# Cross-attention block on one core: all eight W1 blocks by seven products, W2's products summed in shared PSUM banks, joint norm statistics

## The chip, the cores and the metric

The kernel runs on one core of one Trainium2 chip. The metric is device time in microseconds (us) of one execution; the number to predict is the median over several runs. The kernel before has a median of 1502.2 us over three runs (1501.49 to 1502.87).

## The reference: what is computed

`x` and `ctx` hold 128 batches of 128 tokens with 256 features, all float32. There are 16 heads of 16 features, and the feed-forward width is 1024. For each batch:

```python
q = split(x @ Wq + bq);  k = split(ctx @ Wk + bk);  v = split(ctx @ Wv + bv)     # 16 heads
scores = q @ k.T / 4;    scores[j >= i] = -1e30;    attn = softmax(scores)
attn[:, :, 0, :] = 0                                 # row 0 sees nothing
x1  = layer_norm(x + (attn @ v) @ Wo + bo) * g1 + be1
out = layer_norm(x1 + relu(x1 @ W1 + b1) @ W2 + b2) * g2 + be2
```

## The kernel before

Work goes by **pairs** of batches: 64 pairs `p`, 256 tokens each. A pair's way takes six software-pipelined stages, and `step(p)` runs, for `p` = 7 to 63, one stage each of several pairs. On the PE (TensorE) one step does in this order: `weigh(p-2)` (probabilities times values, PSUM tile `pc`), `scores_both(p)` (`pss`), `queries(p+1)` (`pq`), `attention_out(p-2)` (`po`), the keys of `p+1` (`pk`), `values(p)` (`pv`), then `second_by_seven(p-4)` (W2) and `hidden_by_seven(p-3)` (W1). The prologue (`third` to `sixth`) fills the pipeline. Step 63 is the `last` one; its W1 is plain (`hidden`), and behind it `behind(62)`, `behind(63)` and the closing lines run the pairs that are left.

**What sets the order.** The program is put out under a manual schedule: each engine runs its instructions in the order in which the code issues them, and waits by semaphores where a tile is not ready. So where a call stands in `step` decides where its instructions stand in every engine's queue. VectorE is DVE, ScalarE ACT, GpSimd POOL; SP and sometimes ACT issue DMAs.

**Seven products.** A 2x2 block product needs eight block matmuls done plainly. `second_by_seven` (L809) and `hidden_by_seven` (L898) use a Strassen-like scheme: seven products of sums of blocks, with a chain of additions behind. For W2 the sums of the hidden activations are `hS` (`combine_hidden`, POOL, L795 to L798), the sums of weights are `wt`. The seven products go to two PSUM banks, `py` (bank 6, four of them) and `pz` (bank 7, three), each product with four matmuls of 128 columns and with `empty` NOPs between them. When all are done, `sum_of_seven` (DVE, L838 and L846) adds them in five instructions to the residual `x1b` and gives `t2`. For W1, `combine_normed` makes the sums `xS` of the normed tokens (POOL, L866 to L869) and `w1t` holds the weights' sums. The 1024 columns of W1 are eight blocks of 128, four pairs of blocks; `NI = 3` of the pairs go by seven products (21 matmuls of 128 columns, each product in a bank of its own), and blocks 6 and 7 go plainly (L939, four matmuls of 256 columns). The results are added on DVE (`u2`, `u3`, `add2`, `add3`, `add5`: L910 to L924), and ACT applies bias and ReLU block by block. In the profile every float32 matmul shows as two PE instructions, so a product of W2 is a row of `x8`, one of W1 a row of `x6`.

**Round about.** `sums(p, hi, part)` is a reciprocal on DVE (L433) and a normalising multiply on POOL (L434); `turn` transposes the probabilities on DVE (L447), and `bring` moves them by DMA. `turn_x1` transposes the normed tokens (L674) and issues `x1t` and `x1T`, two DMA trips in a row; `combine_normed` waits for `x1T`. Layer-norm statistics are taken for pair `p-2` (first norm) and `p-5` (second norm) apart: each `stats` (L536, L537) on DVE, then `deviation` (L543, L544) and `shift` (L588) on POOL. `residual1` (POOL, L577 and L580) makes `x1b`; `finish` (L608 and L609) closes the second norm.

Of the kernel before, what the change touches and what calls it, by code (L numbers as in the profile page):

```python
# [8 lines left out]
F32 = mybir.dt.float32  # L9
# [4 lines left out]
P = 128  # L14
# [5 lines left out]
def tile_cross_attention_block(  # L20
# [99 lines left out]
    def row(v, name):  # L120
        t = const.tile([P, v.shape[1]], F32, tag=name, name=name)
        nc.sync.dma_start(t, v.to_broadcast([P, v.shape[1]]))
        return t

    load_tokens(0, slice(0, 2))
# [9 lines left out]
    power = const.tile([P, 2, 1], F32, tag="power", name="power")  # L135
# [4 lines left out]
    table = const.tile([P, 2, 1], F32, tag="table", name="table")  # L140
# [11 lines left out]
    be1_r = row(ln1_b, "be1_r")  # L152
    b2_r = row(b2, "b2_r")
# [132 lines left out]
    def copy_keys(p):  # L286
        st = states[p]
        pk = st.pop("pk")
        for m in range(KC):
# [131 lines left out]
    def sums(p, hi, part):  # L421
# [11 lines left out]
        nc.vector.reciprocal(rs, su)  # L433
# [5 lines left out]


# [98 lines left out]
    def deviation(p, i):  # L539
# [4 lines left out]
        nc.gpsimd.tensor_tensor(sd, ve, power, ALU.pow)  # L544
# [28 lines left out]
    def residual1(p, engine=nc.gpsimd):  # L573

        st = states[p]
        x1b = st["x1b"] = ffn.tile([P, 2, D], F32, tag="x1b", name=f"x1b_{p}", bufs=3)
# [46 lines left out]
    b1s = const.tile([P, DFF // NS], F32, tag="b1s", name="b1s")  # L623
# [47 lines left out]
    def turn_x1(p, queue=nc.sync):  # L671
        st = states[p]
        tb = ffn.tile([P, NS, 4 * 32], F32, tag="tbx", name=f"tbx_{p}")
# [63 lines left out]
    def second_sum(p):  # L737
        st = states[p]
        t2 = st["t2"] = ffn.tile([P, 2, D], F32, tag="t2", name=f"t2_{p}", bufs=3)
        nc.vector.tensor_tensor(  # L740
            t2, st.pop("py").rearrange("p (s d) -> p s d", s=2), st.pop("x1b"), ALU.add
        )
# [36 lines left out]
    wt = const.tile([P, 4, FC // 2, P], F32, tag="wt", name="wt")  # L779

    def combine_w2():

        w = w2.rearrange("p (k e) (h d) -> p e h k d", e=2, h=2)
# [16 lines left out]
    def second_by_seven(p):  # L800

        st = states[p]
        hT, hs = st["hT"], st["hS"]
        py = st["py"] = at_bank(6, f"py_{p}")
        pz = st["pz"] = at_bank(7, f"pz_{p}")

        def product(out, left, right, after):
            for k in range(FC // 2):
                nc.tensor.matmul(  # L809
                    out, left(k), right(k), start=(k == 0), stop=(k == FC // 2 - 1)  # L810
                )
                empty(after // (FC // 2) + (after % (FC // 2) > k))

# [6 lines left out]
        product(py[:, :P], raw(0, 0), weights(0, 0), 5)  # L820
        product(pz[:, :P], raw(1, 0), weights(1, 0), 5)
        product(pz[:, 2 * P : 3 * P], raw(1, 1), lambda k: wt[:, 3, k], 5)
# [531 lines left out]
    def step(p):  # L1354
# [55 lines left out]
        if not last:  # L1410
            turn(p, 1, 1)
# [128 lines left out]
```

## Time and profile before

| | before |
|---|---|
| median of three runs | 1502.2 us |
| span of the profiled execution | 1500.2 us |
| mean granted TensorE clock | 0.999 |
| PE busy | 1487.9 us, 99% of the span |
| POOL, DVE, ACT busy | 1357.8, 1334.8, 1290.5 us |

The three runs' times are device times; the profiled execution is shown by its span, from the first to the last instruction, and has no other time of its own on record. The median lies 2.0 us above the span. A step of the steady part lasts 22.80 us, and 56 whole steps (`p` = 7 to 62) lie between 143.54 and 1420.82 us. In the page's rows `xN` counts instructions, the first number behind the bar is busy time, the second the mean duration in ns, and what follows the second bar is idle time before them and its releaser.

### The profile page before, as it was taken

The page shows a single profiled execution, that of the slowest core. Times are in us where ns is not written, and L with a number is a line of the kernel's source. Part 1 is how long each engine was busy: PE and PEld are TensorE (multiplying, and loading weights), DVE is VectorE, ACT ScalarE, POOL GpSimd, SP SyncE. Part 2 cuts the span into 40 slices and gives each one's busy share as a digit, 9 for nine tenths or more (in the row PEclk, how much of TensorE's full clock was granted, in tenths as well). Part 3 has the DMA queues.
Part 4 walks back from the last instruction along what each step waited for, and adds up shares of the span by engine and source line. Part 5 has one row for each costly group of instructions (what it writes and reads, how often), then busy time and mean ns, then how long its engine had stood idle before and what let it go on. Part 6 is the DMA issues. An engine that isn't in the chain of part 4 may idle for free.

```text
span 1500.2 us, 53576 instructions
## 1 busy us (share of the span) xinstructions
PE 1487.9 (99%) x18934; PEld 1366.7 (91%) x18934; DVE 1334.8 (89%) x2663; ACT 1290.5 (86%) x5271; POOL 1357.8 (91%) x1510
## 2 busy tenths in 40 slices
PE   8999999999999999999999999999999999999998
PEld 7788999999999999999999999999999999999997
DVE  6989998998999999999999989989999999899875
ACT  5658988989989989989989899899899899898862
POOL 6878899999999999999999999999999999999983
PEclk9999999999999999999999999999999999999999
DMA  8356656556666566556556565666665565564451
GB/s 200 84 113 143 149 140 137 139 141 140 149 138 142 135 139 145 143 128 146 142 130 156 137 139 136 139 141 147 140 137 139 131 157 142 128 143 128 107 136 49
DMA packets 415317, 204.61 MB, mean 136 GB/s; under 512 B 282449, under 2 KB 383057, under 8 KB 415057
## 3 DMA queue, kind: packets, MB, share of 16 engines
q1 hardware_dynamic: 412768, 199.34, 56.9%
q8 instruction: 158, 2.59, 0.8%
q10 hardware_dynamic: 2288, 1.85, 0.5%
q14 instruction: 103, 0.84, 0.2%
HBM read 70.26 MB, written 33.29 MB: 69 GB/s over the span
## 4 chain that ended last, share of the span: by engine, by line
PE 93%; DVE 3%; POOL 2%; DMA 1%; issue 1%; ACT 1%; SPq 0%; ACTq 0%; POOLq 0%; DVEq 0%
PE phs L898 18%; PE py L809 14%; PE pz L809 10%; PE pq L261 8%; PE pv L301 7%; PE po L523 7%; PE pk L261 7%; PE ph L939 6%; PE pss L384 6%; PE pc L504 4%; PE pc L494 2%; PE ph L710 2%; POOL sm L434 1%; PE py L730 0%; DVE sm L398 0%
## 5 line engine op out<-in xcount | busy, mean ns | idle before, releaser
L775 ACT ACTIVATE sm<-pss,nmx 128x128 f32<-128x128 f32 x944 | 327.8, 402 | 82.5 <-DVE nmx L758 75.5
L434 POOL TENSOR_TENSOR sm<-sm,rs 128x1024 f32<-128x1024 f32 x192 | 361.8, 1899 | 36.4 <-DVE rs L433 33.4
L775 ACT ACTIVATE sm<-sm,nmx 128x64 f32<-128x64 f32 x944 | 313.4, 401 | 0.0
L447 DVE STREAM_TRANSPOSE tb<-sm 128x1024 f32<-128x1024 f32 x186 | 228.1, 1229 | 22.4 <-POOL sm L434 12.0
L775 ACT ACTIVATION_READ_ACCUMULATOR sm<-sm,nmx 128x1 f32 x912 | 231.8, 254 | 0.0
L775 ACT ACTIVATION_READ_ACCUMULATOR sm<-pss,nmx 128x1 f32 x912 | 221.6, 243 | 0.0
L929 ACT ACTIVATE hT<-hT,b1e_c 128x256 f32<-128x256 f32 x336 | 152.1, 501 | 37.0 <-DVE hT L917 37.0
L809 PE MATMUL py<-wt,hS 128*128 128x128 f32 x1440 | 170.7, 275 | 0.0
L809 PEld LDWEIGHTS py<-wt,hS 128*128 128x128 f32 x1440 | 165.6, 192 | 0.0
L758 DVE TENSOR_REDUCE nmx<-pss 128x4 f32<-128x512 f32 x236 | 150.5, 678 | 0.0
L398 DVE TENSOR_TENSOR sm<-pss,neg 128x256 f32<-128x256 f32 (+1 forms) x276 | 107.9, 433 | 40.5 <-PE pss L384 38.9
L898 PE MATMUL phs<-xS,w1t 128*128 128x128 f32 x1008 | 130.9, 275 | 0.0
L291 ACT ACTIVATE kT<-pk,bkh,half 128x256 f32<-128x256 f32 x252 | 123.4, 605 | 4.0 <-PE pk L261 4.0
L261 PE MATMUL pq<-xT,wq 128*128 128x256 f32 x504 | 125.4, 392 | 0.0
L523 PE MATMUL po<-wo,cxT 128*128 128x256 f32 x512 | 121.3, 380 | 0.7 <-ACT cxT L516 0.7
L898 PEld LDWEIGHTS phs<-xS,w1t 128*128 128x128 f32 x1008 | 121.6, 192 | 0.0
L301 PE MATMUL pv<-wv,cT 128*128 128x256 f32 x512 | 121.0, 379 | 0.0
L261 PE MATMUL pk<-cT,wk 128*128 128x256 f32 x504 | 119.2, 379 | 0.0
L523 PEld LDWEIGHTS po<-wo,cxT 128*128 128x128 f32 x512 | 96.9, 190 | 14.5 <-ACT cxT L516 1.3
L301 PEld LDWEIGHTS pv<-wv,cT 128*128 128x128 f32 x512 | 97.2, 190 | 13.2
L261 PEld LDWEIGHTS pq<-xT,wq 128*128 128x128 f32 x504 | 90.7, 189 | 20.2 <-issue 9.8
L261 PEld LDWEIGHTS pk<-cT,wk 128*128 128x128 f32 x504 | 95.7, 190 | 13.1 <-issue 0.2
(165 smaller groups left out, 4085.0 us busy)
## 6 DMA issues: line engine op xcount, KB each, us to landing
pT<-tb SPq DMA_DIRECT2D x976, 96.0 KB, 2.2
x1t<-tbx SPq DMA_DIRECT2D x252, 64.0 KB, 2.9
x1T<-x1t SPq DMA_DIRECT2D x63, 256.0 KB, 3.0
out_dram<-t SPq DMA_DIRECT2D x63, 256.0 KB, 3.2
xb<-in_x_dram SPq DMA_DIRECT2D x124, 128.0 KB, 4.3
cb<-in_ctx_dram SPq DMA_DIRECT2D x124, 128.0 KB, 3.8
x<-in_x_dram SPq DMA_DIRECT2D x31, 512.0 KB, 4.7
w<-in_L_xattn_W_dram SPq DMA_DIRECT2D x2, 1024.0 KB, 8.2
```

The costliest lines, as they stand in the source:

```text
L261: nc.tensor.matmul(ps[:, m * TP : (m + 1) * TP], w[:, k, m * P : (m + 1) * P], src[:, k, :], start=(k == 0), stop=(k == KC - 1),)
L291: nc.scalar.activation(st["kT"][:, m, e, :], pk[:, m * TP : (m + 1) * TP], AF.Identity, bias=bkh[:, m, e : e + 1], scale=half[:, e : e + 1],)
L301: nc.tensor.matmul(pv[:, s * D : (s + 1) * D], st["cT"][:, k, s * P : (s + 1) * P], wv[:, k, :], start=(k == 0), stop=(k == KC - 1),)
L398: nc.vector.tensor_tensor(st["sm", hi][:, 4 * r : 4 * r + 4, :], st["sps", hi][r][:, : 4 * n].rearrange("p (n j) -> p n j", j=n), no[:, No ...
L434: nc.gpsimd.tensor_tensor(sm[:, part, :], sm[:, part, :], rs[:, :, None].to_broadcast([P, part.stop - part.start, n]), ALU.mult,)
L447: nc.vector.transpose(st["tb"][:, :, at : at + 256].rearrange("p j (n a) -> p n j a", a=32), st["sm", hi].rearrange("p h j -> p (h j)")[:, ...
L523: nc.tensor.matmul(po[:, s * D : (s + 1) * D], cxT[:, k, s, :], wo[:, k, :], start=(k == 0), stop=(k == KC - 1),)
L758: nc.vector.tensor_reduce(st["nmx", 1][:, 4 * r : 4 * r + 4], st["sps", 1][r].rearrange("p (n j) -> p n j", j=P), AX.X, ALU.max, negate=True,)
L775: nc.scalar.activation(sm[:, h, :], src, AF.Exp, bias=nmx[:, h : h + 1], scale=1.0, **({"accum_out": st["su", hi][:, h : h + 1]} if summed ...
L809: nc.tensor.matmul(out, left(k), right(k), start=(k == 0), stop=(k == FC // 2 - 1))
L898: nc.tensor.matmul(ps[:, i * P : (i + 1) * P].rearrange("p (n a) -> p n a", a=32), left(i), right, start=True, stop=True,)
L929: nc.scalar.activation(self.hT[:, f], self.plains.get(f, self.hT[:, f]), AF.Relu, bias=b1e_c[:, f : f + 1], scale=1.0,)
```

## The change

- `NI` is 4: all eight W1 blocks go by seven products, 28 matmuls of 128 columns; the plain part is gone. The order of the products is 1, 6, 7, 5, 2, 4, 3. Products 5 and 3 share PSUM bank 2: DVE reads it after 5 (`add5`) and once more after 3 was accumulated onto it (`add3`). Product 4 is in bank 7.
- W2's seven products share three banks: `px` (bank 6) takes three, `py` (bank 7) two, `pz` (bank 3) two side by side. DVE reads a bank midway, before the next product is accumulated onto it, and adds each part at once to the residual tile `t2`, which takes the place of `x1b`: six instructions instead of five.
- The statistics of both norms are one block, `both_stats`: four `bn_stats`, four `bn_aggr`, one `tensor_scalar` and one `scalar_tensor_tensor` on DVE, one power on POOL.
- The order changes: the transposes of the tokens and probabilities stand between the partial sums, `combine_normed` stands ahead of `sums` on POOL, two of the ReLUs go to the start of the next step, and 21 NOPs a step stand where there were 34.
- Some constants share the space of `wt`; `tbx` has one buffer, `t2` four.

```diff
-        def product(out, left, right, after):
+        def product(out, left, right, after, sums, first=False):
             for k in range(FC // 2):
                 nc.tensor.matmul(
-                    out, left(k), right(k), start=(k == 0), stop=(k == FC // 2 - 1)
+                    out, left(k), right(k), start=(first and k == 0), stop=(k == FC // 2 - 1),
+                    skip_group_check=True,
                 )
                 empty(after // (FC // 2) + (after % (FC // 2) > k))
+            for part in sums:
+                others.get(part, lambda: None)()
+                sum_of_seven(p, part)
...
-        product(py[:, :P], raw(0, 0), weights(0, 0), 5)
-        product(pz[:, :P], raw(1, 0), weights(1, 0), 5)
-        product(pz[:, 2 * P : 3 * P], raw(1, 1), lambda k: wt[:, 3, k], 5)
-        product(py[:, 3 * P :], lambda k: hs[:, 0, k], lambda k: wt[:, 0, k], 5)
-        product(py[:, 2 * P : 3 * P], lambda k: hs[:, 2, k], lambda k: wt[:, 2, k], 5)
-        product(py[:, P : 2 * P], lambda k: hs[:, 1, k], lambda k: wt[:, 1, k], 5)
-        product(pz[:, P : 2 * P], lambda k: hs[:, 3, k], weights(1, 1), 4)
+        product(px, raw(0, 0), weights(0, 0), 3, (), True)
+        product(py, lambda k: hs[:, 0, k], lambda k: wt[:, 0, k], 3, (), True)
+        product(pz[:, :P], raw(1, 0), weights(1, 0), 3, (0,), True)
+        product(px, lambda k: hs[:, 1, k], lambda k: wt[:, 1, k], 3, (1,))
+        product(pz[:, P : 2 * P], raw(1, 1), lambda k: wt[:, 3, k], 3, (2,))
+        product(py, lambda k: hs[:, 3, k], weights(1, 1), 3, (3, 4))
+        product(px, lambda k: hs[:, 2, k], lambda k: wt[:, 2, k], 3, (5,))
+    def sum_of_seven(p, part):
+        t = st["t2"].rearrange("p s (h d) -> p (s h) d", h=2)
+        to, of = {
+            0: (t[:, 0], "px"), 1: (t[:, 3], "py"), 2: (t[:, 1], "px"), 3: (t[:, 0:3:2], "pz"),
+            4: (t[:, 1], "py"), 5: (t[:, 2:], "px"),
+        }[part]
...
+        nc.vector.tensor_tensor(to, to, of, ALU.add)
-    NI = 3
+    NI = 4
-        WHERE = {1: 2, 6: 3, 7: 4, 4: 5, 2: 6, 3: 0, 5: 1}
+        WHERE = {1: 2, 6: 5, 2: 6, 7: 3, 4: 7}
+        ONTO = {3: 5}
+        AGAIN = {5: 2}
@@ hidden_by_seven
         h.run(1)
         h.run(6)
         h.keep()
+        copy_keys(p + 1, (1,))
+        h.again()
+        h.u2()
+        spread_values(p)
         stack_values(p)
-        h.u2()
         h.run(7)
-        h.run(4)
+        h.run(5)
         h.u3()
         norm1(p - 2)
+        h.add5()
         h.run(2)
         h.add2()
+        h.run(4)
         h.run(3)
-        h.run(5)
+        norm2(p - 5)
+        h.add4()
         h.relu(0)
         h.relu(2)
         h.relu(4)
-        h.add3()
-        h.add5()
-        h.plain([6], 2)
         h.relu(6)
         turn_x1(p - 2)
-        h.plain([7], 3)
-        norm2(p - 5)
-        h.relu(1)
-        h.relu(7)
+        h.add3()
+        turn(p, 0, 0)
@@ step, the last one (p = 63)
+            sums(p, 1, ONE)
+            sums(p, 1, TWO)
+            shift(p - 5, 2)
+            turn_x1(p - 2)
+            turn(p, 1, 0)
+            second_by_seven(p - 4)
+            residual1(p - 3)
+            sums(p, 0, ALL)
+            turn(p, 1, 1)
+            hidden(p - 3, range(FC))
@@ step, all others
+        joint = both_stats(p)
         sums(p, 1, ONE)
         sums(p, 1, TWO)
+        nc.gpsimd.tensor_tensor(joint[1], joint[1], power, ALU.pow)
+        second_by_seven(p - 4, {
+            1: lambda: (tokens(p + 2, "x") if ahead else None, turn(p, 1, 0)),
+            2: lambda: tokens(p + 2, "c") if ahead else None,
+            3: lambda: (reciprocal(p, 0, ALL), turn(p, 1, 1)),
+            5: lambda: both_shifts(*joint),
+        })
```

Three places show what this does to the engines' queues. The first is the PE at the end of W1 in a steady step, up to the first matmul of the next step's `weigh` (`pc`); `phs_N` is product N of W1 (product 3 runs in the tile of 5), `ph` the plain part, and the brackets name the semaphores waited for. Before:

```order
L898 MATMUL phs_3_12176<-xS_12034,w_127 128x128 [waits Activation_49,Pool_49]
L898 MATMUL phs_3_12176<-xS_12034,w_127 128x128 x2
L898 MATMUL phs_5_12180<-xS_12034,w1t 128x128 [waits Activation_49]
L898 MATMUL phs_5_12180<-xS_12034,w1t 128x128 x2
L939 MATMUL ph_6_12189<-x1T_11802,w_127 128x256 [waits PE_49]
L939 MATMUL ph_6_12189<-x1T_11802,w_127 128x256
L939 MATMUL ph_7_12202<-x1T_11802,w_127 128x256 [waits DVE_49]
L939 MATMUL ph_7_12202<-x1T_11802,w_127 128x256
L494 MATMUL pc_12230<-pT_11820,vd_178 32x64 [waits DMAHW4_49,DMAHW5_49,DMAHW3_49,DMAHW6_49,DMAHW2_49,DMAHW7_49,DMAHW1_49,DMAHW0_49]
```

And in the changed kernel:

```order
L934 MATMUL phs_5_11580<-xS_11381,w1t 128x128 [waits Activation_49]
L934 MATMUL phs_5_11580<-xS_11381,w1t 128x128 x3
L934 MATMUL phs_2_11566<-x1T_11250,w_128 128x128 [waits DVE_49]
L934 MATMUL phs_2_11566<-x1T_11250,w_128 128x128 x3
L934 MATMUL phs_4_11568<-x1T_11250,w1t 128x128 x4
L934 MATMUL phs_5_11580<-xS_11381,w_128 128x128 [waits DVE_49,Pool_49]
L934 MATMUL phs_5_11580<-xS_11381,w_128 128x128 x3
L506 MATMUL pc_11650<-pT_11262,vd_177 32x64 [waits DMAHW4_49,DMAHW3_49,DMAHW5_49,DMAHW2_49,DMAHW6_49,DMAHW1_49,DMAHW7_49,DMAHW0_49,DVE_49]
```

The plain matmuls are gone, each product has a fourth matmul, and `pc` also waits for DVE: its bank 7 holds product 4 until `add4` has read it.

The second place is the PE within W2 of the same step, from the third to the fourth product. Before, the fourth product stands at the place of the first that uses `hS`:

```order
L809 MATMUL py_12067<-wt,hS_11932 128x128 [waits Pool_49]
L215 NO_OP x2
L809 MATMUL py_12067<-wt,hS_11932 128x128
L215 NO_OP
L809 MATMUL py_12067<-wt,hS_11932 128x128
```

In the changed kernel, where `pX` is the tile that three products share:

```order
L842 MATMUL pz_11490<-w_134,hT_11192 128x128
L842 MATMUL pX_11488<-wt,hS_11376 128x128 [waits DVE_49,Pool_49]
L218 NO_OP
L842 MATMUL pX_11488<-wt,hS_11376 128x128
L218 NO_OP
```

The fourth product, D in what follows (A to G in the order of the new code), now waits for DVE too: the first partial sum must have read `pX` before it.

The third place is DVE in the last step, `p` = 63. Before:

```order
L433 RECIPROCAL rs_63_0_24224<-sa_63_24141 128x8
L433 RECIPROCAL rs_63_8_24227<-sa_63_24141 128x8
L674 STREAM_TRANSPOSE tbx_24233<-x_61_24204 128x4x4x32
L447 STREAM_TRANSPOSE tb_24242<-sm_24087 128x8x4x32
L838 TENSOR_TENSOR t_59_24311<-x1b_23935,py_24244 128x512
L838 TENSOR_TENSOR t_59_24311<-t_59_24311,py_24244 128x384
L838 TENSOR_TENSOR t_59_24311<-t_59_24311,py_24244 128x256
L838 TENSOR_TENSOR t_59_24311<-t_59_24311,py_24244 128x2x128
L846 TENSOR_TENSOR t_59_24311<-t_59_24311,pz_24245 128x384
```

And in the changed kernel:

```order
L439 RECIPROCAL rs_63_0_22986<-sa_63_22903 128x8
L439 RECIPROCAL rs_63_8_22989<-sa_63_22903 128x8
L706 STREAM_TRANSPOSE tbx_22995<-x_61_22966 128x4x4x32
L459 STREAM_TRANSPOSE tb_23004<-sm_22849 128x8x4x32
L878 TENSOR_TENSOR t_59_22701<-t_59_22701,pX_23006 128x128
L878 TENSOR_TENSOR t_59_22701<-t_59_22701,py_23007 128x128
L878 TENSOR_TENSOR t_59_22701<-t_59_22701,pX_23006 128x128
L878 TENSOR_TENSOR t_59_22701<-t_59_22701,pz_23008 128x2x128
L878 TENSOR_TENSOR t_59_22701<-t_59_22701,py_23007 128x128
L878 TENSOR_TENSOR t_59_22701<-t_59_22701,pX_23006 128x256
```

The sums stand behind the same two transposes as before; what is new is that the first three of them have to come before products D, F and G.

219 lines of the change are left out of this document (104 added, 115 removed).

## The prediction

> **What bounds the kernel now.** I read the page first, then the table of windows over the steady part, then PE's timeline of one step, then the chain of waits at the end.
>
> ```profile
> span 1500.2 us, 53576 instructions
> PE 1487.9 (99%) x18934; PEld 1366.7 (91%) x18934; DVE 1334.8 (89%) x2663; ACT 1290.5 (86%) x5271; POOL 1357.8 (91%) x1510
> PE 93%; DVE 3%; POOL 2%; DMA 1%; issue 1%; ACT 1%; SPq 0%; ACTq 0%; POOLq 0%; DVEq 0%
> ```
>
> PE is busy 99% of the span and makes up 93% of the chain that ended last. The next rows are windows: the 56 steady steps, then one step cut at the start of its W1.
>
> ```profile
> 143.54:1420.82 1277.28, 1277.27 (x16688) 1187.24 (x16688) 1161.99 (x2351) 1162.43 (x4928) 1195.80 (x1343) 1.00 0.60 139
> 736.80:753.08 16.28, 16.28 (x249) 15.16 (x249) 15.09 (x32) 14.94 (x75) 15.39 (x15) 1.00 0.52 131
> 753.08:759.60 6.52, 6.52 (x53) 6.03 (x51) 5.68 (x12) 5.82 (x16) 5.99 (x11) 1.00 0.82 147
> ```
>
> The columns are length, then busy PE, PEld, DVE, ACT, POOL, the granted clock, DMA. PE is busy 1277.27 of 1277.28 us, so a steady step (1277.28 / 56 = 22.81, 22.80 in this one) is as long as PE's own work; DVE, ACT and POOL each leave 1.4 to 2.1 us of it. So only work taken from PE, or a wait put into PE, moves the time. I write times in a step as an offset from `pc`'s start (here 736.80).
>
> **W1.** PE's timeline of the step:
>
> ```profile
> 729.39 1.06 PE L809 MATMUL pz<-w,hS 128*128 128x128 f32 x8
> 730.28 0.83 PE L898 MATMUL phs<-x1T,w 128*128 128x128 f32 x6
> 734.97 1.89 PE L939 MATMUL ph<-x1T,w 128*128 128x256 f32 x8
> 736.80 0.43 PE L494 MATMUL pc<-pT,vd 128*32 128x64 f32 x16
> 743.38 1.89 PE L261 MATMUL pk<-cT,wk 128*128 128x256 f32 x8
> 745.11 1.89 PE L301 MATMUL pv<-wv,cT 128*128 128x256 f32 x8
> 746.83 1.05 PE L809 MATMUL py<-w,hT 128*128 128x128 f32 x8
> ```
>
> Seven products are 42 PE instructions and take 734.97 - 730.28 = 4.69, or 0.1117 each. The plain part is 8 instructions at (745.11 - 743.38) / 8 = 0.216, or 1.73. Together 6.42; the window is 6.52, so 0.10 is lost at the passage to `pc`. In the change W1 is 56 instructions, 56 x 0.1117 = 6.255; with the same 0.10 it is 6.355. PE saves 0.165 a step and the step falls to 22.64, unless a wait comes in; 56 x 0.165 = **9.2 us**. The NOPs taken out are worth nothing: a W2 product with five of them takes (730.28 - 729.39) / 8 = 0.111 per instruction, what a W1 product takes without any.
>
> **The other engines.** Groups by line and form:
>
> ```profile
> L846 DVE TENSOR_TENSOR t<-t,pz 128x384 f32<-128x384 f32 x60 | 33.2, 554 | 6.8 <-DVE t L838 0.9
> L838 DVE TENSOR_TENSOR t<-t,py 128x256 f32<-128x256 f32 x120 | 50.5, 421 | 4.1
> L536 DVE BATCH_NORM_STATS2 bs<-t 128x6 f32<-128x256 f32 x254 | 101.9, 401 | 2.3
> L537 DVE BATCH_NORM_AGGREGATE mv<-bs 128x2 f32<-128x6 f32 x254 | 46.2, 182 | 8.7
> ```
>
> and one row of DVE's timeline, an addition of 512 columns out of PSUM:
>
> ```profile
> 745.38 0.68 DVE L549 TENSOR_TENSOR t<-po,xb 128x512 f32<-128x512 f32 x1
> ```
>
> The joint statistics take a power, two additions and four products, all a few columns wide, from POOL and give DVE two such instructions. POOL leaves 1.4 us of a step, and PE never stands still in it, so this is worth nothing by itself; what it can do is bring POOL's later work forward. From 384 to 256 columns a sum falls by 0.133, so I put a 128-column part at 0.29: the six parts are 4 x 0.29 + 2 x 0.42 = 2.0 where the five sums were some 2.6. W1's additions grow from 0.55 to 0.68 (384 to 512 columns). DVE stays near 21 of 22.64, ACT is the same but for 0.1. No engine but PE becomes the bound by its work.
>
> **The new waits of a steady step.** Four places on PE now wait for DVE. A starts at offset 10.03 and a product is 0.89, so D is due at 12.7, F at 14.5, G at 15.4. These rows time the inputs:
>
> ```profile
> 740.58 1.27 POOL L795 TENSOR_TENSOR hS<-hT 128x512 f32<-128x512 f32 x1
> 745.61 1.26 POOL L254 TENSOR_TENSOR xb<-x,bov_r 128x512 f32<-128x512 f32 x1
> 747.43 3.75 POOL L434 TENSOR_TENSOR sm<-sm,rs 128x1024 f32<-128x1024 f32 x2 [0.56 <-DVE rs L433]
> 751.14 0.45 POOL L866 TENSOR_TENSOR xS<-x1T 128x128 f32<-128x128 f32 x1
> 741.64 0.38 SPq L242 DMA_DIRECT2D x1T<-x1t  x1
> x1T<-x1t SPq DMA_DIRECT2D x1, 256.0 KB, 3.0
> 749.87 2.59 DVE L447 STREAM_TRANSPOSE tb<-sm 128x1024 f32<-128x1024 f32 x2 [0.22 <-DMA pT<-tb]
> ```
>
> - D waits for part 0. DVE has `t1` by 9.3, the joint statistics take 4 x (0.40 + 0.18) = 2.3, part 0 ends at 11.9: slack 0.8.
> - F waits for part 1, behind the probabilities' transpose, which waits for POOL. POOL starts `hS` at 3.8 to 3.9 and is through its four at 8.9 (745.61 - 740.58 = 5.03). `combine_normed` now stands there and needs `x1T`: issued at 4.84, landing 3.0 later at 7.9, so no wait; it is done at 10.7, the first multiply at 12.6, the transpose (2.59 / 2) at 13.9, part 1 at 14.3. Slack 0.2.
> - G waits for part 2, one token transpose (512 columns, some 0.6 by the 2.59 for 2048) and 0.29 later than part 1, at 15.2: slack 0.2.
> - `pc` waits for `add4`. Product 4 is the sixth of seven: its last instruction starts at 16.28 + 47 x 0.1117 = 21.53 and lasts 0.28 (row below), `add4` takes 0.68: 22.5, against 22.64. Slack 0.1.
>
> ```profile
> L898 PE MATMUL phs<-xS,w1t 128*128 128x128 f32 x1008 | 130.9, 275 | 0.0
> ```
>
> No row has these waits, so I bound them: no stall at all, or, if each hand-over takes 0.1 more than I allow, up to 0.13 at `pc`, 7.3 us in all. A stall at F, G or `pc` holds back all that PE does next, in the order `pc`, `pss`, `pq`, so it comes back every step. I take no stall, as all four slacks are positive; the gain lies between 1.9 and 9.2.
>
> **The last step.** Here the new waits are not short. Rows of PE, DVE and POOL around it:
>
> ```profile
> 1430.15 2.84 PE L809 MATMUL py<-wt,hS 128*128 128x128 f32 x24
> 1433.72 7.07 PE L710 MATMUL ph<-x1T,w 128*128 128x256 f32 x32
> 1434.24 3.75 POOL L434 TENSOR_TENSOR sm<-sm,rs 128x1024 f32<-128x1024 f32 x2
> 1434.16 0.71 DVE L674 STREAM_TRANSPOSE tbx<-x 128x512 f32<-128x512 f32 x1 [1.47 <-ACT x L565]
> 1436.17 1.25 DVE L447 STREAM_TRANSPOSE tb<-sm 128x1024 f32<-128x1024 f32 x1 [1.30 <-POOL sm L434]
> ```
>
> D is due at 1430.15. But on DVE the parts stand behind two transposes, of which one waits for ACT until 1434.16 and one for POOL until 1436.17; it ends at 1437.42. Part 0 ends at 1437.71, and D starts at 1437.75: PE stands still for **7.6 us**. Before, the same order cost nothing, since PE waited for no sum and went on with L710. Everything behind it on PE (three products, W1 of pair 60, the epilogue) moves by that, and it isn't given back: PE's rows from there to its last matmul follow each other nearly without a gap.
>
> Behind it the same waits cost less. Rows of the end:
>
> ```profile
> 1439.69 2.62 ACT L718 ACTIVATE hT<-ph,b1e_c 128x256 f32<-128x256 f32 x7
> 1474.16 1.22 PE L809 MATMUL py<-w,hT 128*128 128x128 f32 x8
> 1475.23 0.70 DVE L795 TENSOR_TENSOR hS<-hT 128x512 f32<-128x512 f32 x1 [1.20 <-ACT hT L718]
> 1477.17 0.69 DVE L798 TENSOR_TENSOR hS<-hT,hS 128x512 f32<-128x512 f32 x1
> 1480.71 1.53 PE L710 MATMUL ph<-x1T,w 128*128 128x256 f32 x6
> ```
>
> In `behind(62)`, part 0 stands behind four `hS` and the statistics of pair 59: the ReLUs, now right behind PE, end 1.1 after W1; the four `hS` take some 2.6 (1475.23 to 1477.86 in a later row), the statistics 2 x (0.40 + 0.18) = 1.2, part 0 0.3: 5.1, where D is due 4.2 after W1: **+0.9**. In `behind(63)` ACT's eight DMA issues hold the time and I put the change at **-0.2**. In the closing W2, B needs the first `hS`, done at 1475.93, 0.9 behind its due time of 1475.05; and part 0 comes behind the last `hS` (1477.86). That is D at 1478.2 where it would be 1476.84, less the 0.3 that this W2 already loses (1480.71 - 1474.16 = 6.55 against 6.25): **+1.0**.
>
> **The clock behind a long pause.** The last matmul starts from `py_last` (first row); the windows are of the tail; the last row is from the start:
>
> ```profile
> 1487.69 7.07 PE L1491 MATMUL py_last<-w,hT 128*128 128x256 f32 x32
> 1497.00:1498.50 1.50, 0.00 (x0) 0.00 (x0) 0.41 (x1) 0.00 (x0) 0.00 (x0) 1.00 0.13 46
> 1498.50:1500.20 1.70, 0.00 (x0) 0.00 (x0) 0.00 (x0) 0.00 (x0) 0.00 (x0) 0.53 0.12 42
> 6.59 3.78 PE L984 MATMUL pk<-cT,wk 128*128 128x256 f32 x8
> ```
>
> PE ends at 1494.76; the granted clock is 1.00 until 1498.50, 3.7 us on, and 0.53 after. At the start, behind idle time, 8 instructions take 3.78 where they take 1.89 later: half pace for about 3.6 us (6.59 to 10.17). A pause of 7.6 us is past that 3.7, so I add half of 3.6, **+1.8**; between 0 (no loss on return) and 5 (half of the program's first 10.2 us, if half pace held all that time).
>
> The Trainium skill's page "TensorE: Matmul & The Clock Gate", Part 1, states the same gate: after an idle window of about 3.4 us the clock passes every second pulse, until the PE was busy for such a window again. By its figure the pause would cost an estimated 1.7 us, and its table of rules speaks against any pause over some 3 us between bursts, as this change makes one. The trace agrees as to the fall (3.7 us); no row of it shows a return in the midst of a program, and the clock column reads 1.00 at the start, where the matmuls take twice as long.
>
> **The sum.** 1500.2 - 9.2 + 7.6 + 0.9 - 0.2 + 1.0 + 1.8 = 1502.1. The prologue (four sums of W1's weights a third wider, on POOL) I put at nothing, as POOL runs ahead there. The median of runs lies 2.0 above the profiled span, so **1504.1 us**. What this kernel's measurement can tell from no change is 0.2%, 3.0 us: 1499.2 to 1505.2.
>
> **Rivals.**
> 1. *The midway chain is late in each steady step.* F has 0.2 of slack behind five links (`hS`, `x1T`, `combine_normed`, multiply, transpose), `pc` 0.1 behind `add4`. It decides from the point where the links together take 0.25 more than summed. At 0.4 more, 0.2 x 56 = 11.2 are lost: 1515. For it: POOL now has `combine_normed` and two multiplies in a row ahead of the transpose, and the `x1T` landing varies with the DMA load. Against it: POOL's 5.99 of 6.52 in W1 came from work that is now elsewhere or gone. Chance 0.15; with half of it, 1510.
> 2. *The stall at 63 is smaller or made up for.* If ACT's and POOL's rows came 5 us earlier, or the epilogue absorbed it, 1504.1 - 7.6 - 1.8 = 1494.7. Against it: the two releasers do not depend on W2. Chance 0.07.
> 3. *The 0.10 at the passage to `pc` goes away too*, as the matmuls ahead of it are narrow now: 56 x 0.10 = 5.6 more, 1498.5. For it: this is the only gap in the step. Against it: the same passage stays (a narrow 32-row `pc` behind full tiles), with one wait more. Chance 0.13.
> 4. *The clock does not fall*: 1502.3. Chance 0.15.
>
> My forecast has 0.50: gain and loss nearly cancel. Within it, the small stalls at `pc` (0 to 7.3) and the upper bound of the clock reach up to 1511, so a good third of it lies above 1505.2. Alone it would be 1502 to 1509. Range: from 1496 (most of rival 3 and part of 2) to 1512 (half of rival 1). Faster: rivals 2 and 3 and a little, 0.22. Slower: rival 1 (0.15) and 0.2 of the forecast's, 0.35. Same: 0.43.
>
> **What would show it.** Right: 56 steps of 22.64 with PE busy throughout, W1 at 6.36, and one pause of 7.6 on PE in the last step, released by DVE's first partial sum, with a lower granted clock behind it. Wrong: PE waits for DVE at F or `pc` in each step (rival 1); no pause, or a short one, near 1430 (rival 2); W1 at 6.26 (rival 3); full pace right behind the pause (rival 4).

## The result, and the profile after

The changed kernel takes 1528.43 us in the median of four runs (1526.44 to 1529.95); the kernel before 1501.85, also in four. The ratio is 1.0178, 95% interval 1.0164 to 1.0193: **1.8% slower**, where I had forecast no change (1504.1). The profiled span is 1526.8 us, 26.6 above that of before.

The page of the changed kernel, its head and its chain:

```profile
span 1526.8 us, 53815 instructions
PE 1500.5 (98%) x19270; PEld 1387.0 (91%) x19270; DVE 1368.1 (90%) x2835; ACT 1313.8 (86%) x5271; POOL 1258.1 (82%) x1118
PE 92%; DVE 3%; ACT 1%; issue 1%; POOL 1%; DMA 1%; SPq 0%; POOLq 0%; DVEq 0%; ACTq 0%
```

This looks like before, and it misleads: PE seems as busy as it was, though it has less to do. Cutting the program at the starts of `pc` (from the trace's records) shows where the time went:

| us | before | after | difference |
|---|---|---|---|
| up to the start of step 7 | 143.54 | 144.10 | +0.6 |
| 56 steps (7 to 62) | 1277.3 | 1292.8 | +15.5 |
| the last step (63) | 19.90 | 29.06 | +9.2 |
| pair 62's stage behind it | 16.63 | 17.32 | +0.7 |
| the rest | 42.86 | 43.52 | +0.7 |

The end, from the last step on, is 10.5 us longer; the forecast's terms for it make 11.1. The start says little: over the kernels of this study it varies from 141.25 to 144.69. The steady part is not as forecast: I had it 9.2 us faster, and it is 15.5 slower. One steady step in windows (length, busy PE, PEld, DVE, ACT, POOL, clock, DMA), and its W1 alone:

```profile
721.43:744.51 23.08, 23.01 (x305) 21.55 (x305) 21.45 (x46) 21.17 (x89) 19.62 (x18) 1.00 0.58 133
738.16:744.51 6.35, 6.35 (x58) 6.23 (x57) 4.82 (x11) 5.02 (x13) 5.00 (x5) 1.00 0.76 131
```

W1 takes 6.35, as worked out. So the 0.44 us by which the step misses 22.64 lie ahead of it. PE's timeline of W2 in this step, the products A to G and W1's first:

```profile
731.47 1.05 PE L842 MATMUL pX<-w,hT 128*128 128x128 f32 x8
732.36 1.06 PE L842 MATMUL py<-wt,hS 128*128 128x128 f32 x8
733.25 1.06 PE L842 MATMUL pz<-w,hT 128*128 128x128 f32 x8
734.38 1.13 PE L842 MATMUL pX<-wt,hS 128*128 128x128 f32 x8
735.35 1.06 PE L842 MATMUL pz<-wt,hT 128*128 128x128 f32 x8
736.30 1.13 PE L842 MATMUL py<-w,hS 128*128 128x128 f32 x8
737.27 1.06 PE L842 MATMUL pX<-wt,hS 128*128 128x128 f32 x8
738.16 1.06 PE L934 MATMUL phs<-x1T,w 128*128 128x128 f32 x8
```

A, B and C follow each other by 0.89. D starts 1.13 after C: 0.24 late. Then E is 0.08 late against D, F 0.06 against E, and G 0.08 against F. That is 0.46 together, 0.44 in the mean of the 56 steps. D and F wait for a sum, and E and G take over 0.07 to 0.08 from them: in the median of the steps D starts 0.146 after the end of part 0, and F 0.146 after the end of part 1. A product's row is 1.06 long and the next begins 0.89 after it, so a pause of up to 0.17 leaves no gap in the busy time; that is why PE counts 23.01 busy of 23.08. The table of waits shows it only under the weight loads, with no releaser named (total, times, longest):

```profile
PEld pX L842 <- issue: 17.0, 53, 4.8
```

DVE's timeline from the statistics to part 1 (the addition of `py`), and the group of the long row:

```profile
732.10 0.33 DVE L569 BATCH_NORM_AGGREGATE mv<-bsb 128x2 f32<-128x6 f32 x4
732.46 1.59 DVE L572 TENSOR_SCALAR sd<-mv 128x4 f32<-128x4 f32 x1
733.96 0.27 DVE L878 TENSOR_TENSOR t<-t,pX 128x128 f32<-128x128 f32 x1
734.16 0.70 DVE L250 STREAM_TRANSPOSE xT<-xb 128x512 f32<-128x512 f32 x1
734.79 1.20 DVE L459 STREAM_TRANSPOSE tb<-sm 128x1024 f32<-128x1024 f32 x1
735.91 0.25 DVE L878 TENSOR_TENSOR t<-t,py 128x128 f32<-128x128 f32 x1
```

```profile
L572 DVE TENSOR_SCALAR sd<-mv 128x4 f32<-128x4 f32 x56 | 87.0, 1554 | 1.9
```

The addition of epsilon to four numbers per partition, one of those that I had called "a few columns wide", takes 1.55 us in the mean. At the end of the same program, with POOL idle, such an addition to one number per partition takes 0.15 (L1525, at 1519.07). With 0.16, part 0 could start at some 732.7; it starts at 733.96, and part 1 stands behind it in DVE's queue. POOL in that time:

```profile
732.13 3.75 POOL L440 TENSOR_TENSOR sm<-sm,rs 128x1024 f32<-128x1024 f32 x2
```

and, in a window that begins later, its second multiply alone:

```profile
733.98 1.90 POOL L440 TENSOR_TENSOR sm<-sm,rs 128x1024 f32<-128x1024 f32 x1
```

The first multiply runs from 732.13 to 734.03; the `tensor_scalar` ends at 734.05. This is no accident of one step: in all 56, POOL is at work when the `tensor_scalar` starts, and its end lies 0.022 to 0.027 us behind the end of that POOL instruction. Its own length varies from 0.28 to 1.82 with it. The same holds for the `scalar_tensor_tensor` of the shifts (L576), 0.015 to 0.019 behind in all 56, though it loses less. The statistics, the reciprocals and the transposes on DVE keep their lengths beside POOL: in the 56 steps `bn_stats` takes 0.41 to 0.42, the reciprocal of 128x8 0.18 to 0.19, the transpose of the probabilities 1.18 to 1.25.

In the last step PE stands still twice:

```profile
1444.44 1.06 PE L842 MATMUL py<-wt,hS 128*128 128x128 f32 x8
1448.01 1.16 PE L842 MATMUL pz<-w,hT 128*128 128x128 f32 x8 [2.51 <-ACT sm L805]
1453.85 2.05 PE L842 MATMUL pX<-wt,hS 128*128 128x128 f32 x8 [4.68 <-DVE t L878]
1455.69 1.65 PE L842 MATMUL pz<-wt,hT 128*128 128x128 f32 x8
```

C waits for ACT, since its bank 3 still holds scores that the exponentials read, and D for part 0. D and E then run at half pace. The granted clock in windows (the third column from the end):

```profile
1448.00:1450.00 2.00, 1.16 (x8) 0.97 (x8) 0.73 (x5) 1.96 (x6) 1.74 (x5) 1.00 0.66 158
1450.00:1452.00 2.00, 0.00 (x0) 0.00 (x0) 0.71 (x1) 2.00 (x13) 2.00 (x2) 0.52 0.63 154
1456.00:1458.00 2.00, 2.00 (x16) 2.00 (x16) 0.64 (x2) 0.00 (x0) 1.27 (x1) 0.77 0.17 34
```

### The profile page after: what moved, and what is told of

It reads as the page before. It is cut to its first block, busy times and chain, and to the rows that moved or that the text cites. A ratio compares the mean times of both kernels' runs of the same rounds, so it can differ in the third digit from the quotient of the medians.

```text
span 1526.8 us, 53815 instructions
## 1 busy us (share of the span) xinstructions
PE 1500.5 (98%) x19270; PEld 1387.0 (91%) x19270; DVE 1368.1 (90%) x2835; ACT 1313.8 (86%) x5271; POOL 1258.1 (82%) x1118
## 4 chain that ended last, share of the span: by engine, by line
PE 92%; DVE 3%; ACT 1%; issue 1%; POOL 1%; DMA 1%; SPq 0%; POOLq 0%; DVEq 0%; ACTq 0%
PE phs L934 23%; PE pX L842 11%; PE pq L264 7%; PE py L842 7%; PE pz L842 7%; PE po L535 7%; PE pv L304 7%; PE pk L264 7%; PE pss L387 6%; PE pc L516 3%; PE ph L742 3%; PE pc L506 2%; ACT hT L750 1%; ACT sm L805 0%; PE py L762 0%
## 5 line engine op out<-in xcount | busy, mean ns | idle before, releaser
L459 DVE STREAM_TRANSPOSE tb<-sm 128x1024 f32<-128x1024 f32 x186 | 223.5, 1204 | 3.3 <-POOL sm L440 3.3
L965 ACT ACTIVATE hT<-hT,b1e_c 128x256 f32<-128x256 f32 x448 | 191.1, 499 | 19.2 <-DVE hT L956 19.1
L934 PE MATMUL phs<-xS,w1t 128*128 128x128 f32 x1344 | 159.2, 275 | 0.0
L934 PEld LDWEIGHTS phs<-xS,w1t 128*128 128x128 f32 x1344 | 154.6, 192 | 0.0
L640 POOL TENSOR_TENSOR t<-t,g_r 128x512 f32<-128x512 f32 x62 | 80.2, 1294 | 84.1 <-ACT t L634 83.9
L827 POOL TENSOR_TENSOR hS<-hT 128x512 f32<-128x512 f32 x57 | 72.3, 1268 | 87.5 <-ACT hT L965 86.4
L842 PE MATMUL pX<-wt,hS 128*128 128x128 f32 x960 | 131.9, 281 | 9.5 <-DVE t L878 5.5
L842 PEld LDWEIGHTS pX<-wt,hS 128*128 128x128 f32 x960 | 117.3, 193 | 18.7 <-issue 17.0
L294 ACT ACTIVATE kT<-pk,bkh,half 128x256 f32<-128x256 f32 x252 | 130.6, 588 | 4.0 <-PE pk L264 4.0
L934 PE MATMUL phs<-x1T,w 128*128 128x128 f32 x896 | 118.3, 275 | 0.0
```

Source lines behind the costliest of these rows:

```text
L294: nc.scalar.activation(st["kT"][:, m, e, :], pk[:, m * TP : (m + 1) * TP], AF.Identity, bias=bkh[:, m, e : e + 1], scale=half[:, e : e + 1],)
L459: nc.vector.transpose(st["tb"][:, :, at : at + 256].rearrange("p j (n a) -> p n j a", a=32), st["sm", hi].rearrange("p h j -> p (h j)")[:, ...
L842: nc.tensor.matmul(out, left(k), right(k), start=(first and k == 0), stop=(k == FC // 2 - 1), skip_group_check=True,)
L934: nc.tensor.matmul(ps[:, i * P : (i + 1) * P].rearrange("p (n a) -> p n a", a=32), left(i), right, start=(i == 0 and which not in self.ONT ...
L965: nc.scalar.activation(self.hT[:, f], self.hT[:, f], AF.Relu, bias=b1e_c[:, f : f + 1], scale=1.0,)
```

## The experiments

**Theory 1**: DVE's `tensor_scalar` is held until the POOL instruction that runs has ended; part 0 and D come late by it; nothing else is wrong in the steady step. **Rival 2**: D loses the time because it waits for two semaphores. **Rival 3**: DVE's queue is too long there, whatever the instruction. Each ratio below is to runs of the kernel before that were taken with it. In the edits `...` stands for lines that are not shown.

### e1: epsilon on POOL

```diff
-        nc.vector.tensor_scalar(sd, mv[:, :, 1:2], LN_EPS, None, ALU.add)
...
+        nc.gpsimd.tensor_scalar(joint[1], joint[0][:, :, 1:2], LN_EPS, None, ALU.add)
         nc.gpsimd.tensor_tensor(joint[1], joint[1], power, ALU.pow)
```

> The changed kernel with one edit: the addition of epsilon (128x4, L572) goes from DVE to POOL, ahead of the power there. Theory 1 (DVE's tensor_scalar is held until POOL's running multiply ends, 1.59 us, and so part 0 and PE's product D come late): D starts 0.89 us behind C, the steady step falls from 23.08 to 22.64 to 22.70, the median to 1503 to 1507 us. Rival 2 (a matmul that waits for two semaphores, DVE and POOL, loses 0.24 us by itself): D stays 0.24 late, the step 23.0 or more, the median above 1522.

Measured: 1504.11 us, ratio to before 1.0013 (1.0004 to 1.0022). One steady step in windows, and its third and fourth product:

```profile
710.54:733.18 22.64, 22.64 (x306) 21.40 (x305) 20.19 (x45) 21.15 (x89) 19.83 (x19) 1.00 0.62 150
```

```profile
722.37 1.06 PE L841 MATMUL pz<-w,hT 128*128 128x128 f32 x8
723.26 1.06 PE L841 MATMUL pX<-wt,hS 128*128 128x128 f32 x8
```

D starts 0.89 behind C, though it waits for the same two semaphores: rival 2 falls. F and G follow on time too (0.894 and 0.895 in the mean). One instruction of 128x4 on DVE cost 24 us; with it on POOL the kernel has the time that I had forecast for the change, which is partly luck (see below).

### e2: epsilon on DVE, as a reduction

```diff
...
-        nc.vector.tensor_scalar(sd, mv[:, :, 1:2], LN_EPS, None, ALU.add)
+        nc.vector.tensor_reduce(sd, mv3[:, :, 1:3], AX.X, ALU.add)     # column 2 of mv3 holds LN_EPS
```

> The changed kernel with one edit: the addition of epsilon stays on DVE, at the same place and size, but as a tensor_reduce over the variance and a constant column beside it. Theory 1 (it is the tensor_scalar's way of reading SBUF that POOL's instruction holds up): the instruction takes 0.1 to 0.3 us instead of 1.59, the step is 22.64 to 22.75, the median 1503 to 1509. Rival 3 (DVE's queue is too long there, whatever the form of the instruction): the step stays at 23.0 or more, the median above 1522. Rival 2 (two waits on D): as rival 3.

Measured: 1504.85 us, ratio 1.0019 (1.0008 to 1.0029). The group:

```profile
L579 DVE TENSOR_REDUCE sd<-mv 128x4 f32<-128x8 f32 x56 | 9.0, 161 | 1.9
```

Same engine, same place, one input of twice the size: 0.161 us instead of 1.554. Rival 3 falls: it is the form of the instruction.

### e3: the tensor_scalar behind part 0

```diff
-        nc.vector.tensor_scalar(sd, mv[:, :, 1:2], LN_EPS, None, ALU.add)     # in both_stats
...
-            1: lambda: (tokens(p + 2, "x") if ahead else None, turn(p, 1, 0)),
+            1: lambda: (nc.vector.tensor_scalar(joint[1], joint[0][:, :, 1:2], LN_EPS, None, ALU.add),
+                        tokens(p + 2, "x") if ahead else None, turn(p, 1, 0)),
...
```

> The changed kernel with one edit: the tensor_scalar stands on DVE behind part 0 of W2's sum, no longer ahead of it; POOL's power moves behind with it. Theory 1: it is still held until POOL's multiply ends (within 0.03 us of it), but part 0 is early now and D starts 0.89 behind C; the transposes behind it are as late as before, so F loses 0.1 to 0.4; step 22.75 to 23.0, median 1509 to 1522. Rival 2 (two waits on D): D stays 0.24 late. Rival 3 (queue too long): part 0 early, the tensor_scalar short (0.3 or less), and F late all the same.

Measured: 1518.21 us, ratio 1.0105 (1.0088 to 1.0123). DVE, and then products E and F:

```profile
728.32 0.29 DVE L877 TENSOR_TENSOR t<-t,pX 128x128 f32<-128x128 f32 x1 [0.20 <-PE pX L841]
728.53 1.20 DVE L1442 TENSOR_SCALAR sd<-mv 128x4 f32<-128x4 f32 x1
```

```profile
730.73 1.06 PE L841 MATMUL pz<-wt,hT 128*128 128x128 f32 x8
731.78 1.13 PE L841 MATMUL py<-w,hS 128*128 128x128 f32 x8
```

Part 0 is early now and D on time. The `tensor_scalar` is still held (its ends lie 0.023 to 0.030 behind POOL's), all that stands behind it is late, and F starts 1.05 behind E instead of 0.89. The step is 22.88: the wait went from D to F, where it costs half.

### e7: POOL's multiply in four

```diff
-        sums(p, 1, ONE)
+        sums(p, 1, ONE, 4)      # the multiply on POOL as four instructions of two heads each
...
```

> The changed kernel with the tensor_scalar where it was, and POOL's first multiply of the probabilities cut in four, so that POOL runs four short instructions there for one of 1.90 us. Theory 1 (the hold lasts as long as the POOL instruction that runs): the tensor_scalar takes 0.15 to 0.65 us, its ends lie 0.02 to 0.03 behind the end of a quarter, D is on time, the step 22.64 to 22.80, the median 1503 to 1512. Rival 3 (DVE's queue or the instruction itself): still 1.5 to 1.6 us and 23.0 or more.

Measured: 1515.38 us, ratio 1.0083 (1.0064 to 1.0101). DVE's group; POOL's row of the four quarters and the second multiply; E and F on PE:

```profile
L575 DVE TENSOR_SCALAR sd<-mv 128x4 f32<-128x4 f32 x56 | 17.1, 306 | 1.9
```

```profile
727.93 4.18 POOL L443 TENSOR_TENSOR sm<-sm,rs 128x256 f32<-128x256 f32 x5
```

```profile
730.85 1.06 PE L845 MATMUL pz<-wt,hT 128*128 128x128 f32 x8
731.86 1.13 PE L845 MATMUL py<-w,hS 128*128 128x128 f32 x8
```

The `tensor_scalar` shrinks from 1.554 to 0.306 with nothing changed on DVE, ending 0.023 to 0.028 behind a quarter: the hold lasts as long as POOL's instruction. D is on time. I missed the price of the cut: the four quarters and the second multiply take 4.18 us where two multiplies took 3.75, the transpose behind the quarters starts 3.01 behind A where it is 2.57 in e1, and F is late (1.01 behind E). That is the place and the mechanism of the prediction's first rival: with 0.4 more in that chain, the step is 22.85 and the median 1515.4, where that rival had put it at 1515.

### e8: two inputs in SBUF

```diff
...
-        nc.vector.tensor_scalar(sd, mv[:, :, 1:2], LN_EPS, None, ALU.add)
+        nc.vector.tensor_tensor(sd, mv[:, :, 1:2], eps, ALU.add)
```

> The changed kernel with the addition of epsilon on DVE, at the same place and size, as a tensor_tensor of the variance and a constant column, both in SBUF. If what POOL holds up is any DVE instruction that reads SBUF twice over, as the scalar_tensor_tensor of the shifts is held too (its ends lie 0.015 to 0.019 behind POOL's in all 56 steps of the changed kernel): 1.5 to 1.6 us, the step 23.0 to 23.1, median 1526 to 1530. If only the tensor_scalar is held: 0.1 to 0.3 us, the step 22.64 to 22.75, median 1503 to 1509.

Measured: 1528.72 us, ratio 1.0174 (1.0158 to 1.0191), as the changed kernel.

```profile
L575 DVE TENSOR_TENSOR sd<-mv,eps 128x4 f32<-128x4 f32 x56 | 88.2, 1576 | 1.9
```

So not the `tensor_scalar` alone: a `tensor_tensor` with both inputs in SBUF is held too (0.015 to 0.020 behind POOL's ends). The sums of W2 and W1 have two inputs as well, but one of them in PSUM, and they are not held: in all steady steps W1's take 0.65 to 0.69 and W2's of 128 columns 0.24 to 0.29.

### e5: the cost by itself, in the kernel before

```diff
...
+        if not last:
+            nc.vector.tensor_reduce(probed[:, :, 0:1], probe, AX.X, ALU.add)
+            nc.vector.tensor_scalar(probed[:, :, 1:2], probe[:, :, 1:2], LN_EPS, None, ALU.add)
```

> The kernel before, with two tiny instructions more on DVE in each steady step, behind the token transposes, while POOL is within its first multiply: a tensor_reduce of 128x8 to 128x4, then a tensor_scalar of 128x4 as in the changed kernel; their output is not used. Theory 1 (a tensor_scalar is held until POOL's running instruction ends): the tensor_reduce takes 0.1 to 0.2 us, the tensor_scalar 0.5 to 0.9, and its ends lie 0.02 to 0.03 behind POOL's in every step; DVE's later work shifts by some 0.8, so 0 to 0.3 a step, median 1502 to 1519. Rival (it was something of the changed kernel's order, not the instruction): both take 0.1 to 0.2, the median stays within 1500 to 1504.

Measured: 1504.57 us, ratio 1.0015 (1.0006 to 1.0024). The two groups:

```profile
L1409 DVE TENSOR_SCALAR probed<-probe 128x4 f32<-128x4 f32 x56 | 44.2, 790 | 0.0
L1408 DVE TENSOR_REDUCE probed<-probe 128x4 f32<-128x8 f32 x56 | 6.7, 119 | 0.0
```

In another kernel, at a place of my choice, the one is held for 0.79 us (in 55 of 56 steps POOL was at work, and the end lies 0.023 to 0.026 behind POOL's; in the one step where POOL was idle it takes 0.16), the other is not. It costs the kernel only 0.06 a step: there DVE has slack, since PE waits for no sum midway.

### e4, e6, e9, e10: the end

In e4 the partial sums of the last step go ahead of what they stood behind, and the third bank is one whose scores are read earlier.

```diff
...
+            second_by_seven(p - 4, {
+                2: lambda: attention_sum(p - 2),
+                3: first_stats,          # statistics and norm 1 of pair 61
+            }, 1)                        # pz in bank 1
             stats(p - 5, states[p - 5]["t2"], 2)
...
             sums(p, 1, ONE)
             sums(p, 1, TWO)
             turn_x1(p - 2)
             turn(p, 1, 0)
-            second_by_seven(p - 4)
```

> The changed kernel with another order in the last step alone (pair 63): W2's partial sums stand on DVE ahead of the statistics, the reciprocals and the two transposes, and the third bank of its products is bank 1, whose scores are read earlier than those of bank 3. Steady steps are as in the changed kernel. If the pause of 7.2 us in PE there and the half clock behind it (3.3 us for two products instead of 1.8) are the last step's whole loss and are not given back: 8 to 9.5 us less, median 1519 to 1520.5. If the epilogue takes the pause over at another place: less than 4 us.

Measured: 1525.85 us, ratio 1.0150 (1.0129 to 1.0171); 2.6 us below the changed kernel, not 8 to 9.5. The intervals of the two ratios overlap; in the profiles, the time from the last step to the end is 86.8 for 89.9. The last step itself is 19.90 us long again, as before. But in the stage behind it:

```profile
1458.78 1.39 PE L842 MATMUL pX<-w,hT 128*128 128x128 f32 x8
1463.89 2.05 PE L842 MATMUL py<-wt,hS 128*128 128x128 f32 x8 [3.73 <-DVE hS L827]
```

```profile
1461.93 1.25 DVE L459 STREAM_TRANSPOSE tb<-sm 128x1024 f32<-128x1024 f32 x1 [3.44 <-POOL sm L440]
1463.10 0.65 DVE L827 TENSOR_TENSOR hS<-hT 128x512 f32<-128x512 f32 x1
```

My new order put POOL's multiplies later, the low transpose waits for the last of them, `hS` stands behind that transpose, and B waits for `hS`, again with the half clock behind it. The pause was carried over, as the second case of the expectation has it.

e6 is e1 with this order and a mended stage behind it: the transpose behind `hS`, all its DMAs on SP, the products in the order A C E B D F G.

```diff
...
-            turn(p, 0, 0)                                  # in the last step
...
+        def older():                                       # in behind(62), ahead of part 2
+            turn(p + 1, 0, 0)
+            bring(p + 1, nc.sync, LATE_FIRST)
...
+        second_by_seven(p - 2, {2: older} if p == NP - 2 else {}, 3, True)
```

> The changed kernel with epsilon added on POOL (as in e1) and the end put in order: in the last step the partial sums ahead of the statistics, the transposes and the exponentials of norm 1's rows, bank 1 for the third bank; the last low transpose behind the sums of hidden activations, its DMAs all on SP; in the three W2 stages behind the last step the order of the products is A C E B D F G. If the pause of the last step and what the epilogue does with it are all that is left above the kernel before: steady step 22.64, no pause over 1 us in PE behind pair 63's scores, no half clock; span 1491 to 1493, median 1493 to 1495, 0.5 to 0.6% faster than before. If the pause moves on once more: 1498 to 1502.

Measured: 1498.16 us, ratio 0.9977 (0.9967 to 0.9986): faster than before, but less than hoped; span 1495.4. PE, DVE and POOL in that stage:

```profile
1439.39 1.16 PE L841 MATMUL pX<-wt,hS 128*128 128x128 f32 x8 [2.93 <-DVE t L881]
```

```profile
1432.85 1.58 DVE L826 TENSOR_TENSOR hS<-hT 128x512 f32<-128x512 f32 x1
1434.36 2.38 DVE L827 TENSOR_TENSOR hS<-hT 128x512 f32<-128x512 f32 x1
1436.66 1.75 DVE L828 TENSOR_TENSOR hS<-hS,hT 128x512 f32<-128x512 f32 x1
```

```profile
1433.84 2.36 POOL L440 TENSOR_TENSOR sm<-sm,rs 128x1024 f32<-128x1024 f32 x1
1436.16 1.70 POOL L257 TENSOR_TENSOR xb<-x,bov_r 128x512 f32<-128x512 f32 x1
```

The same hold, both ways: the three `hS` take 1.58, 2.38 and 1.75 where they take 0.65 to 0.70 alone, and POOL's multiply 2.36 instead of 1.90, its addition 1.70 instead of 1.27. The second `hS` starts at 1434.36, POOL's multiply ends at 1436.20, and `hS` ends 0.54 after that: the two take turns.

e9 brings POOL's multiplies and the residual forward.

```diff
...
+                2: lambda: (attention_sum(p - 2), sums(p, 1, ONE)),
+                3: lambda: stats(p - 2, states[p - 2]["t1"], 1),
+                5: lambda: sums(p, 1, TWO),
...
```

> As e6, with POOL's multiplies and the residual of the last step brought forward (the reciprocals ahead of the statistics), so that POOL is idle when DVE makes the sums of hidden activations behind it, and with the last low transpose behind part 2. In e6 these sums took 1.58, 2.38 and 1.75 us instead of 0.65 while POOL ran, and D waited 2.93 us. If that is the same hold between DVE and POOL: the three sums take 0.6 to 0.7 us, D waits less than 0.5, span 1490.5 to 1493, median 1493 to 1495.5, 0.4 to 0.6% faster than the kernel before. If the wait has another cause (ACT's ReLUs, PE's order): D still waits over 2 us, median as e6's, 1497.5 to 1499.

Measured: 1498.97 us, ratio 0.9982 (0.9973 to 0.9991): no better than e6. D's wait fell to 0.94, but POOL's low multiply still lay on the first `hS` (1.40 us) and its addition for pair 63 on the second (1.76). The transpose, now later still, held up the DMAs of pair 63's probabilities: SP issued them one behind the other from 1441.40 on, for 10.07 us, and the last of them landed at 1453.05, 0.44 ahead of `pc`. The row below names the transpose of the tokens, `tbx`, but that had ended at 1452.64.

```profile
1453.49 0.43 PE L506 MATMUL pc<-pT,vd 128*32 128x64 f32 x16 [3.18 <-DVE tbx L705]
```

e10 puts the low multiply ahead of pair 58's statistics on POOL, POOL's addition for pair 63 behind `hS`, and the transpose ahead of `hS`.

```diff
...
             sums(p, 0, ALL)
+            deviation(p - 5, 2)
+            shift(p - 5, 2)
             turn_x1(p - 2)
             hidden(p - 3, range(FC))
+            turn(p, 0, 0)
+            bring(p, nc.sync, LATE_FIRST)
...
```

> As e9, with POOL's low multiply of pair 63 ahead of the statistics of pair 58, POOL's addition for pair 63 moved behind the sums of hidden activations, and the last low transpose ahead of these sums, so that its DMAs start some 6 us earlier. In e9 PE waited 0.94 us for a sum and 3.18 us for the probabilities of pair 63. If both waits come from POOL's work lying on DVE's and from the late transpose: neither is over 0.4, span 1490.5 to 1493, median 1492.5 to 1495.5, 0.4 to 0.6% faster than the kernel before. If PE waits move on once more: 1497 or more.

Measured: 1494.55 us (1494.0 to 1494.86), ratio 0.9947 (0.9933 to 0.9961), span 1493.1: **0.5% faster than the kernel before** and the fastest version of this study. DVE, and what is left on PE:

```profile
1434.86 0.65 DVE L826 TENSOR_TENSOR hS<-hT 128x512 f32<-128x512 f32 x1
1435.43 0.68 DVE L827 TENSOR_TENSOR hS<-hT 128x512 f32<-128x512 f32 x1
```

```profile
1450.51 0.43 PE L506 MATMUL pc<-pT,vd 128*32 128x64 f32 x16 [0.94 <-issue]
```

With POOL's multiply and addition out of the way the `hS` take 0.65 to 0.69 again and D does not wait. POOL is not idle there; now it is the one held: two `nb`, that take 0.50 elsewhere, take 1.96 from 1434.88 on, and its addition behind them 1.76 instead of 1.27. That costs nothing, as PE waits for neither. A pause of 0.94 is left ahead of pair 63's `pc`, over twice the 0.4 that I had allowed. Its row names no releaser, but the last of the probabilities' DMAs lands at 1450.10, 0.41 ahead of it, as in e9 (0.44).

Two numbers per kernel, both in us, from the starts of `pc`: the mean of the 56 steady steps, and what the program takes from the start of the last step (63) to its end:

| kernel | steady step | last step to the end |
|---|---|---|
| before | 22.81 | 79.4 |
| after | 23.09 | 89.9 |
| e1, epsilon on POOL | 22.65 | 90.1 |
| e2, by a reduction | 22.67 | 91.2 |
| e3, behind part 0 | 22.88 | 90.8 |
| e4, last order | 23.09 | 86.8 |
| e5, probe in before | 22.87 | 79.2 |
| e6 | 22.66 | 84.2 |
| e7, multiply in four | 22.85 | 90.7 |
| e8, two inputs | 23.10 | 91.2 |
| e9 | 22.65 | 85.1 |
| e10 | 22.65 | 80.1 |

## Why the prediction was wrong

- **The step that failed** is the first of the four midway waits, "D waits for part 0 ... slack 0.8". It priced the joint statistics by `bn_stats` and `bn_aggr` rows (2.3 us) and the `tensor_scalar` at nothing. Those rows were, if anything, dear: from the first `bn_stats` to the last `bn_aggr` the changed kernel needs 1.7. But the `tensor_scalar` took 1.55, because POOL was within a 1.90 us multiply, and part 0 ended 0.24 too late for D. Part 1, behind it in the queue, ended 0.06 too late for F, and each of the two waits passed some 0.07 on. That made 0.44 a step, 24.5 us by the spans of the changed kernel and e1. e1, e2 and e7 take the long `tensor_scalar` away by three different edits and D is on time in each.
- The sentence on the joint statistics, "give DVE two such instructions", had the mechanism at hand and didn't ask what these two share with POOL. In the steady part of before no row shows it: there, DVE's instructions read one operand from SBUF, or one from SBUF and one from PSUM. In its prologue two rows of DVE do: beside POOL at work, two `tensor_scalar` of 128x256 (L569, at 62.69 and 63.89) take 1.28 and 1.36 us, and each ends 0.15 behind the end of a POOL instruction (63.82 and 65.10). At its end one row of POOL does, the other way round: two `nb` that take 0.50 elsewhere lie among DVE's `hS`. I passed over all of them.

```profile
1460.27 1.99 POOL L588 TENSOR_SCALAR nb<-mv,sd 128x1 f32<-128x1 f32 x2
```

- The Trainium skill has the rule. Its page "SBUF — State Buffer", section "Who interferes with whom", says that DVE and GpSimd share a second pair of SBUF ports, that `tensor_scalar` can need it in its fast modes and a DVE instruction with two SBUF inputs needs it against a GpSimd instruction that reads SBUF, and: "Whoever issues first gets the shared pair for the whole instruction; the other fully blocks (not throttle)." It also says that `tensor_reduce` never contends on this chip. The runs agree on all three: 1.554 (`tensor_scalar`) and 1.576 us (two inputs) against 0.161 (`tensor_reduce`). No run shows the ports themselves, nor in which mode the `tensor_scalar` ran.
- **The W1 saving** was right: W1 6.35 (forecast 6.355), steady step 22.64 in e1, 8.8 us over the 56 steps with the longer first of them (forecast 9.2). The 0.10 at the passage to `pc` stayed, so the third rival fell.
- **F, G and `pc`**: without the `tensor_scalar` on DVE none of them waits in a usual step of e1, so slacks of 0.1 to 0.2 were enough. The first rival was right that the midway chain decides, and on the side of slower; it named F and `pc`, where it was D, and F only behind it. e3 and e7 show that F is next: 0.4 more in its chain costs 0.2 a step.
- **The last step**: forecast 7.6, measured 1453.85 - (1443.55 + 3 x 0.893) = 7.6, but as two pauses. That C has to wait 2.5 us for ACT in bank 3 I had not seen; part 0 was later, so the sum hid it. The second rival fell: in the changed kernel nothing gave it back. What e4 adds is that an order which frees the sums delays other work; only e10 recovers 9.6 us of it (1504.11 to 1494.55).
- **Behind it**: pair 62's W2 takes 7.11 from A to `po` (1467.44 to 1474.55) where it took 6.43, +0.7 for the +0.9 forecast; in pair 63's stage 6.36 for 6.70, -0.3 for -0.2; the closing W2 7.63 for 6.55, +1.1 for +1.0.
- **The clock**: D and E take 3.32 where two products take 1.79, +1.5 for the +1.8 forecast. The granted clock was 0.5 from 1450.1 to 1456.9, so the fourth rival fell. The estimate from the Trainium skill's page "TensorE: Matmul & The Clock Gate", Part 1, was 1.7. Its "idle window" of about 3.4 us doesn't fit as it stands: the 3.4 us before the fall held 1.16 us of work.
- So without the held instruction the span is 1502.3 (e1), where the sum had been put at 1502.1. That it comes this close is partly luck: the saving is 0.4 smaller and the end, 10.7 in e1 for 11.1, 0.4 smaller as well, and the start alone varies by more. **The range** was too narrow at its upper end, since each of the midway waits was allowed only 0.1 us more per hand-over, and no term for an instruction that is held.

## What to carry to other kernels

Before an instruction is put on DVE beside a busy POOL, look at what it reads: in these runs a `tensor_reduce`, a reciprocal, a statistic or a transpose with one SBUF input, or an addition with one of its two inputs in PSUM, cost its own time; a `tensor_scalar` from SBUF or a form with two SBUF inputs cost what was left of POOL's instruction, however small it was. All of these POOL instructions read SBUF; others were not tried. Where PE waits for a sum midway, everything ahead of that sum in DVE's queue is on PE's path, so price each instruction there at its worst. A pause shorter than the overlap of two matmul rows doesn't show in PE's busy time: compare the starts of the products.

## What the runs showed of the hardware that I had not expected

- An instruction on four columns lasted up to 1.82 us, its end 0.022 to 0.027 us behind the end of POOL's instruction in all 56 steps; and POOL is held by DVE in turn (2.36 instead of 1.90 us in e6).
- The clock fell at about 1450.1, 0.9 us after product C had ended (1449.17) and with 1.16 us of work in the 3.4 us before it: a short burst between two pauses did not keep it up. It was back at about 1456.9, 3.0 us after D had started.
- A product behind a pause is 1.13 long in its row instead of 1.06 and passes 0.07 to 0.08 on to the next: a wait of 0.24 cost 0.32.
